# Cross-attention on one core: ten copies of the last batch's value tile move from VectorE to transfers of the sync engine

## The chip, the cores and the metric

One core of a Trainium2 chip runs the whole program in one launch. The metric is the time of an execution on the device in microseconds (us), lower is better. The engines are TensorE (PE in the profile; its weight loads are PEld), VectorE (DVE), ScalarE (ACT), GpSimd (POOL) and SyncE (SP, which only issues transfers). Each has its own instruction queue and works through it in order; semaphores tie them together.

## The reference

For each of 32 batches `x` and `y` (the context) are 256 x 1024, fp32, and all weights are 256 x 256:

```python
x_q = einsum('oc,bcn->bno', w_qk, y)
x_k = einsum('oc,bcn->bon', w_qk, x)
x_v = einsum('oc,bcn->bon', w_v, x) + b_v[None, :, None]
energy = einsum('bnc,bcm->bnm', x_q, x_k)
attention = softmax(energy, axis=-1)
attention = attention / (1e-07 + attention.sum(axis=1, keepdims=True))
x_r = einsum('bcn,bnm->bcm', x_v, attention)
x_r = relu(einsum('oc,bcn->bon', w_t, x - x_r) + b_t[None, :, None])
return x + x_r
```

## The kernel before

The weights are folded once at the start: `g` (w_qk transposed times w_qk) and `wvtT` (values and output projection in one). Every large product is a 2 x 2 block product of 128 x 512 blocks, done with seven block products in place of eight (class `Seven`: `p1` to `p7` are the products, `c11`, `c12`, `c21`, `c22` the combinations). The operands of the seven products are blocks of a tile and sums of blocks, and the sums are tiles of their own (`xs`, `ys`, `gt`, `us`, `et`).

One batch b has four stages:

- Keys (`Keys`, matmuls into `pg`): `gx` = g times x. GpSimd makes its block sums `gt`.
- Values (`Values`, matmuls into `pu`): `ut`, 128 x 2 x 2 x 512 fp32. The product that uses it needs it turned inside each 128 x 128 square. `turn` (line 366) transposes 32 x 32 squares with four VectorE instructions into `turned`; then each of the 16 pairs (partition group a, column group g) must be copied from one group of 32 partitions to another, back into `ut`. That copy is `move` (line 374): it takes the next `count` pairs off a list and issues one copy of 32 x 16 x 32 elements for each with whatever issuing function it is given. GpSimd then makes the block sums `us` in four instructions (`factors`, line 383), each 128 x 512.
- Energy (`Energy`, matmuls into `pe`), for t = 0 to 3: the energies of two row tiles go to `e` with their row minimum or maximum (custom VectorE instructions, `combine`, line 412), ScalarE takes the exponential (`exp`, line 436), and VectorE adds the rows, scaled, into `acc` (`share`, line 450). The 128 x 1024 `acc` instruction reads two tiles in SBUF. `columns` and `inverse` (lines 595 and 609) make the column factors `rc` of `acc`.
- Attention (`Attention`, matmuls into `po`): `e` times `rc` (`normal`), block sums `et` (`mix`), the products with `ut` and `us` (`epart`, line 489), and the output blocks `z`, stored by SP (`store`, line 505).

The stages of neighbouring batches overlap. The order of the instructions on PE, DVE, ACT and POOL is that of the program text (`InOrder`, lines 66 to 82, hangs each instruction behind the one before it on its engine); SP's transfers are put by the tile scheduler. The value tile of batch b+1 is made and turned at the end of batch b's attention (`now.run(un)`, line 783; its last call is `u.turn()`, line 571). The 16 copies are shared out in three ways:

- first batch: all 16 by SP transfers, line 680
- batches 1 to 30: eight by VectorE (line 790), eight by ScalarE (lines 670 and 684)
- batch 31, the last: twelve by VectorE (line 790, called at the end of batch 30's pass) and four by ScalarE (line 722, in t = 0 of batch 31's energies)

The matmuls of batch 31 that wait for these tiles are in `run` (line 533): `epart(self.one, 1)`, line 548, is the first to read the copied part of `ut_31`, and `epart(self.three, 2)`, line 550, comes after it; the sums `us_31` are first read by `epart(self.two, 5)`, line 551. In between lie all four steps of batch 31's energies, `columns` and `inverse`. In the last batch no loads are left.

The names used below: `pe` and `po` are PSUM banks of energies and attention; `ep1s`, `ep5s` and `ew` are ScalarE's copies of a bank that PE then adds onto; `nm` and `bias` are row extremes; `ri` is the reciprocal of a row sum. Almost every line of an engine with `InOrder` shows as L77, so instructions are told apart by their tiles.

Of the kernel before, what the change touches and what calls it, by code (L numbers as in the profile page):

```python
# [16 lines left out]
def kernel(  # L17
# [29 lines left out]
    nc = tc.nc  # L47
    B, C, N = x.shape
# [33 lines left out]
    pe, dve, act, pool = (InOrder(g) for g in (nc.tensor, nc.vector, nc.scalar, nc.gpsimd))  # L82
# [6 lines left out]
    def load(tag, b, pieces=1):  # L89
        from_, p = (x, xp) if tag == "x" else (y, yp)  # L90
        to = p.tile([P, KC, N], F32, tag=tag, name=f"{tag}_{b}")
        from_ = from_[b].rearrange("(k p) n -> p k n", p=P)
        W = KC // pieces
        for j in range(pieces):
            nc.sync.dma_start(to[:, ts(j, W)], from_[:, ts(j, W)])
        loaded[tag, b] = to
# [127 lines left out]
    def summed(tag, b):  # L224


        p = up if tag == "x" else one
        s = p.tile([P, 4, MB], F32, tag=f"{tag}s", name=f"{tag}s_{b}")
        t1, t3, t4, t2 = (s[:, j] for j in range(4))
        to = loaded[tag, b]  # L230
        b11, b12 = to[:, 0, ts(0, MB)], to[:, 0, ts(1, MB)]
        b21, b22 = to[:, 1, ts(0, MB)], to[:, 1, ts(1, MB)]
        if b == 0:
            pool.tensor_tensor(t1, b11, b12, ALU.add)
            pool.tensor_tensor(t2, b22, t1, ALU.add)
            pool.tensor_tensor(t3, b12, b22, ALU.add)
            pool.tensor_tensor(t4, b21, t2, ALU.add)
            steps = []
        else:
            from_ = (x if tag == "x" else y)[b]  # L240
            q = quarters(from_)
            nc.sync.dma_start(s[:, :2], q[:, 0, 1:2, :].to_broadcast([P, 2, MB]))
            nc.sync.dma_start(s[:, 2:], q[:, 1])
            steps = [
                lambda: accumulate(s[:, :2], corners(from_)),
                lambda: accumulate(s[:, 2:], s[:, 0:1].to_broadcast([P, 2, MB])),
                lambda: accumulate(t4, q[:, 1, 1]),
            ]
        return (b11, b21, b22, t4, t1, t2, t3), steps
# [345 lines left out]
    def columns(b):  # L595

        dve.tensor_reduce(
            parts[:, :, 0],
            acc.rearrange("p (j r) -> p j r", r=G32),
            AX.X,  # L600
            ALU.add,
            apply_transpose=True,
        )
# [5 lines left out]
    def inverse(b):  # L609


        sc = one.tile([P, NB, 1], F32, tag="sc", name=f"sc_{b}")
        s = sc[:, :, 0]
        for a in range(1, NG):
            moved(parts[:G32, :, a], parts[ts(a, G32), :, 0])
        dve.tensor_reduce(s[:G32], parts[:G32], AX.X, ALU.add)
        dve.reciprocal(s[:G32], s[:G32])
        moved(s[G32 : 2 * G32], s[:G32])
        moved(s[2 * G32 :], s[: 2 * G32])
        rc = one.tile([P, NB, G32], F32, tag="rc", name=f"rc_{b}")  # L620
        dve.transpose(rc.rearrange("p j r -> p (j r)"), sc.to_broadcast([P, NB, G32]))
        return rc.rearrange("p j r -> p (j r)")
# [27 lines left out]
    u = Values(0, xr)  # L650
# [11 lines left out]
    for b in range(B):  # L662
        more = b + 1 < B
        pair = []

        for t in range(HT):
            now = Energy(b, t, lhs, rhs)
            pair.append(now)
            if t == 0 and b > 0 and more:
                u.move(5, act.copy)  # L670
            now.p1()
            if t > 0:
                pair[t - 1].exp(1)
            now.p5()
            if t == 0:
                if b == 0:
                    u.p4()
                    u.c21()
                    u.turn()
                    u.move(16, nc.sync.dma_start)  # L680
                    xsteps[1]()
                    xsteps[2]()
                elif more:
                    u.move(3, act.copy)
                    before.end()
                    before.c21()
                    load("x", b + 1)
                e = ep.tile([P, NT, N], F32, tag="e", name=f"e_{b}")
                acc = one.tile([P, N], F32, tag="acc", name=f"acc_{b}")
                if before is not None:  # L690

                    pool.tensor_copy(behind, before.t4[:, HT - 1, :1])
                for step in gsteps:
                    step()
                if more:
                    ur, usteps = u.factors()
                    for step in usteps:
                        step()
            if t > 1:
                pair[t - 2].share(0)  # L700
            if t == 0:
                now.p6()
            now.p2()
            now.c11()
            if t == 1:
                pair[0].scale(1)
            if t > 1:
                pair[t - 1].share(1)
            if t > 0:
                now.p6()  # L710
            if t == 1:
                act.activation(acc, e[:, HT, :], AF.Copy, scale=scales[HT])
            if t > 0:
                pair[t - 1].p4()
                pair[t - 1].c21()
                pair[t - 1].exp(0)
            now.p3()
            now.c12()
            now.p7()
            now.c22()  # L720
            if t == 0 and not more:
                u.move(4, act.copy)
                ur, usteps = u.factors()
                for step in usteps:
                    step()
            elif t == 0 and b > 0:
                xn, xsteps = summed("x", b + 1)
            elif more and b > 0:
                xsteps[t - 1]()
        last = pair[-1]  # L730

        if more:
            g = Keys(b + 1, xn)
            g.p1()
        last.exp(1)
        if more:
            g.p5()
        else:
            before.xpart(before.one, 7, True)
        pair[2].share(0)  # L740
        last.p4()
        last.c21()
        last.share(1)
        if more:
            load("y", b + 1)
            rhs, ysteps = summed("y", b + 1)
            g.p6()
        else:
            before.epart(before.one, 7)
        last.exp(0)  # L750
        if more:
            g.p2()
            g.c11()
            g.p3()
        else:
            now = Attention(b, xr, ur)
            now.begin()
        last.share(0)
        columns(b)
        if more:  # L760
            g.p7()
            g.c12()
            g.c22()
            un = Values(b + 1, xn)
            un.p1()
            un.p5()
            un.p2()
            un.p6()
        else:
            before.c22()  # L770
        rc = inverse(b)
        if more:
            un.p3()
            g.p4()
            g.c21()
            un.p7()
            lhs, gsteps = g.factors()

        if more:
            now = Attention(b, xr, ur)  # L780
            now.begin()
            ysteps[0]()
            now.run(un)
            if b + 2 < B:
                now.xpart(now.one, 7, True)
                now.epart(now.one, 7)
                now.c22()
                now.put()
            now.put()
            un.move(8 if b + 2 < B else 12, dve.tensor_copy)  # L790
            ysteps[1]()
            ysteps[2]()
            before = now
            xr, u = xn, un
        else:
            before.end()
            now.run(None, before)
            now.finish()
# [30 lines left out]
```

## Time and profile before

| | |
|---|---|
| time, median of 3 runs | 2143.03 us (2142.68 to 2144.03) |
| the profiled execution's own time | 2142.41 us |
| its span (first to last instruction) | 2140.6 us, so 1.8 us lie around it |
| mean granted TensorE clock | 0.999 |
| ScalarE copies of `ut` | 244, median 615 ns |
| VectorE copies of `ut` | 252, median 417 ns |
| SP transfers of `ut` (first batch) | 16, issue 619 to 1668 ns, landing 2.7 to 5.4 us after issue |
| GpSimd instructions for `us` | 128, four to a batch |

A busy share is an average over the whole span. A single stage is read from the timeline: each line gives the start, the length, the engine, the line, the operation with its output and inputs, and how often it comes in a row; in square brackets stands the idle time of the engine before it and what ended it. One fp32 matmul of 128 x 128 by 128 x 512 is two MATMUL records, and at full clock one such pair starts 0.86 us after the last. `SPq` is SP's queue of transfers; a length there is the time to issue, not to move.

### The profile page before, as it was taken

Reading aid. Unit: us, or ns where it says so; the run is one execution under the profiler, and the core shown is the slowest. Engines: PE = TensorE matmul, PEld = TensorE weight load, DVE = VectorE, ACT = ScalarE, POOL = GpSimd, SP = SyncE. Lnnn points to the kernel's source line nnn. Section 1 sums busy time; section 2 is a strip of 40 time slices with the busy share of each in tenths; the row PEclk is TensorE's granted clock in tenths of the full one; section 3 lists DMA queues with packets and bytes.
Section 4 is the critical chain, followed back from the end, with each engine's and each line's share of the span. In section 5 each row is a group of like instructions: output and inputs, shape, how many; then the busy total and the mean of one; then the engine's idle time right before and its main releaser. Section 6 shows DMA issues by size and latency. Waiting matters only on the chain.

```text
span 2140.6 us, 17690 instructions
## 1 busy us (share of the span) xinstructions
PE 2130.6 (100%) x4972; PEld 941.3 (44%) x4972; DVE 1907.8 (89%) x3499; ACT 944.2 (44%) x1566; POOL 549.8 (26%) x487
## 2 busy tenths in 40 slices
PE   9999999999999999999999999999999999999999
PEld 5444444444444444444444444444444444444433
DVE  6899888998888988889888899888998888988898
ACT  5344554335543355433455344553345543355432
POOL 4322323222222122221222322323222222122220
PEclk9999999999999999999999999999999999999999
DMA  6445544445444454444554445554445444454420
GB/s 177 99 107 118 135 131 103 117 104 138 128 108 125 92 143 125 117 122 97 129 133 125 108 111 118 132 134 103 114 108 138 128 108 124 93 143 123 116 66 30
DMA packets 114210, 249.94 MB, mean 117 GB/s; under 512 B 17088, under 2 KB 17856, under 8 KB 114112
## 3 DMA queue, kind: packets, MB, share of 16 engines
q1 hardware_dynamic: 71456, 167.53, 23.6%
q0 software_dynamic: 42656, 81.28, 23.4%
q8 instruction: 40, 0.66, 0.1%
q14 instruction: 58, 0.48, 0.1%
HBM read 181.67 MB, written 33.55 MB: 101 GB/s over the span
## 4 chain that ended last, share of the span: by engine, by line
PE 97%; DVE 3%; issue 0%; ACT 0%; DVEq 0%
PE po L77 43%; PE pe L77 35%; PE pg L77 9%; PE pu L77 9%; DVE e L77 1%; DVE acc L77 0%; DVE et L77 0%; DVE ut L77 0%; PE idle L77 0%; DVE z L77 0%; DVE rc L77 0%; DVE parts L77 0%; DVE turned L77 0%; DVE sc L77 0%; DVE gx L77 0%
## 5 line engine op out<-in xcount | busy, mean ns | idle before, releaser
L77 PE MATMUL pe<-gt,ys 128*128 128x512 f32 x768 | 392.1, 592 | 0.0
L77 PE MATMUL po<-et,us 128*128 128x512 f32 x768 | 347.5, 594 | 1.1 <-DVE et L77 1.1
L77 DVE SCALAR_TENSOR_TENSOR e<-e,ri,rc 128x512 f32<-128x512 f32 x512 | 347.4, 747 | 1.1
L77 DVE SCALAR_TENSOR_TENSOR acc<-e,ri,acc 128x1024 f32<-128x1024 f32 x224 | 289.0, 1290 | 8.0
L77 PE MATMUL pe<-gx,y 128*128 128x512 f32 x512 | 261.4, 592 | 0.0
L77 PEld LDWEIGHTS pe<-gt,ys 128*128 128x128 f32 x768 | 146.0, 190 | 184.4 <-issue 182.6
L77 PEld LDWEIGHTS po<-et,us 128*128 128x128 f32 x768 | 143.1, 190 | 189.8 <-issue 145.9
L77 PE MATMUL po<-e,ut 128*128 128x512 f32 x512 | 224.9, 592 | 0.0
L77 ACT COPY ut<-turned 32x512 f32<-32x512 f32 x244 | 150.0, 615 | 157.4 <-DVE turned L77 154.6
L77 ACT ACTIVATE e<-e,nm 128x1024 f32<-128x1024 f32 x128 | 147.1, 1149 | 98.1 <-DVE nm L77 96.2
L77 POOL TENSOR_TENSOR gt<-gx 128x512 f32<-128x512 f32 x64 | 80.9, 1264 | 383.1 <-DVE gx L77 383.1
L77 DVE TENSOR_TENSOR et<-e 128x1024 f32<-128x1024 f32 x128 | 153.7, 1222 | 2.3
L77 PEld LDWEIGHTS po<-e,ut 128*128 128x128 f32 x512 | 97.3, 190 | 122.5 <-issue 99.0
L77 PEld LDWEIGHTS pe<-gx,y 128*128 128x128 f32 x512 | 97.3, 190 | 122.5 <-issue 122.2
L77 ACT ACTIVATE e<-e,bias 128x1024 f32<-128x1024 f32 x128 | 147.4, 1152 | 5.6 <-DVE bias L77 5.4
L77 DVE CUSTOM_DVE_ANT_0 e<-pe,ep1s 128x512 f32<-128x512 f32 x128 | 88.5, 691 | 64.1 <-ACT e L77 63.1
L77 PE MATMUL pe<-gx,ys 128*128 128x512 f32 x256 | 131.6, 596 | 3.5 <-DVE nm L77 3.5
L77 POOL TENSOR_TENSOR us<-ut 128x512 f32<-128x512 f32 x64 | 82.0, 1282 | 206.2 <-ACT ut L77 192.4
L77 PE MATMUL pe<-gt,y 128*128 128x512 f32 x256 | 131.7, 596 | 0.1
L77 ACT COPY ep1s<-pe 128x512 f32<-128x512 f32 x128 | 74.5, 582 | 114.5 <-PE pe L77 107.2
L77 PE MATMUL po<-e,us 128*128 128x512 f32 x256 | 120.5, 592 | 0.0
L77 DVE CUSTOM_DVE_ANT_0 e<-pe,zeros,nm 128x512 f32<-128x512 f32 x128 | 95.7, 748 | 27.3 <-PE pe L77 26.1
(118 smaller groups left out, 3200.4 us busy)
## 6 DMA issues: line engine op xcount, KB each, us to landing
y<-in_ctx_dram SPq DMA_DIRECT2D x32, 1024.0 KB, 4.9
out_dram<-z SPq DMA_DIRECT2D x128, 256.0 KB, 2.1
x<-in_x_dram SPq DMA_DIRECT2D x31, 1024.0 KB, 5.8
xs<-in_x_dram SPq DMA_DIRECT2D x62, 512.0 KB, 4.6
ys<-in_ctx_dram SPq DMA_DIRECT2D x62, 512.0 KB, 4.7
xs<-in_x_dram POOLq DMA_DIRECT2D x31, 512.0 KB, 6.3
xs<-xs POOLq DMA_DIRECT2D x31, 512.0 KB, 5.0
ys<-in_ctx_dram POOLq DMA_DIRECT2D x31, 512.0 KB, 6.2
```

The source lines that it names most:

```text
L77: self.last = getattr(self.engine, name)(*args, **kwargs)
```

## The change

In the last batch ten of the sixteen copies go from VectorE to SP. VectorE keeps two, ScalarE keeps its four. The other 31 batches are as before. In the compiled program PE, DVE, ACT and POOL keep their order, apart from the ten copies that are gone from DVE. SP gets ten transfers: one ahead of the store of output block z_0_1 of batch 30, nine behind it. The first `us` instruction of batch 31 on POOL, and the first matmul on PE that reads the moved part of `ut_31`, now wait for semaphores of transfers too.

```diff
@@ -720,6 +720,7 @@
             now.c22()
             if t == 0 and not more:
                 u.move(4, act.copy)
+                u.move(10, nc.sync.dma_start)
                 ur, usteps = u.factors()
                 for step in usteps:
                     step()
@@ -787,7 +788,7 @@
                 now.c22()
                 now.put()
             now.put()
-            un.move(8 if b + 2 < B else 12, dve.tensor_copy)
+            un.move(8 if b + 2 < B else 2, dve.tensor_copy)
             ysteps[1]()
             ysteps[2]()
             before = now
```

## The prediction

> **What bounds the kernel now.** The summary first: busy times of PE and DVE, and the engines of the chain of waits.
>
> ```profile
> PE 2130.6 (100%) x4972; PEld 941.3 (44%) x4972; DVE 1907.8 (89%) x3499; ACT 944.2 (44%) x1566; POOL 549.8 (26%) x487
> PE 97%; DVE 3%; issue 0%; ACT 0%; DVEq 0%
> ```
>
> TensorE bounds nearly everything, but 31 batches stay as they are, so only the 70 us after batch 31's value tile is turned count. Their timeline, without weight loads:
>
> ```profile
> 2070.24 2.50 ACT L77 COPY ut<-turned 32x512 f32<-32x512 f32 x4 [0.85 <-DVE turned L77]
> 2070.64 5.15 DVE L77 COPY ut<-turned 32x512 f32<-32x512 f32 x12
> 2073.75 1.02 PE L77 MATMUL pe<-gt,ys 128*128 128x512 f32 x2
> 2075.82 0.69 DVE L77 CUSTOM_DVE_ANT_0 e<-pe,ep1s 128x512 f32<-128x512 f32 x1
> 2078.08 1.82 PE L77 MATMUL pe<-gx,ys 128*128 128x512 f32 x2 [3.31 <-DVE nm L77]
> 2079.40 0.56 ACT L77 COPY ep5s<-pe 128x512 f32<-128x512 f32 x1
> 2080.01 1.99 PE L77 MATMUL pe<-gt,y 128*128 128x512 f32 x2
> 2081.84 1.02 PE L77 MATMUL pe<-gt,ys 128*128 128x512 f32 x2
> ```
>
> The reader is to see one stall. DVE copies for 5.15 us before it touches batch 31's energies; PE cannot overwrite a bank that DVE has not read, stands idle for 3.31 us, and then runs its next two products at half speed (1.82 and 1.99 in place of 1.02). The windows give the clock (length, busy times of PE, PEld, DVE, ACT and POOL, clock, transfers):
>
> ```profile
> 2074.00:2078.00 4.00, 0.78 (x2) 0.00 (x0) 3.77 (x11) 0.00 (x0) 1.99 (x2) 1.00 0.00 0
> 2078.40:2081.70 3.30, 3.19 (x4) 0.84 (x3) 1.41 (x5) 3.30 (x6) 2.61 (x3) 0.50 0.00 0
> ```
>
> From there the chain of waits, in order of time, goes PE, DVE, PE without slack:
>
> ```profile
> 2080.01 11.45 PE pe L77 x24
> ...
> 2105.94 6.72 DVE e L77 x10
> ...
> 2116.65 19.84 PE po L77 x44
> ```
>
> So what PE gains at 2081.84 reaches the end, unless DVE, saturated from 2091.59 on, is made later.
>
> **The ten copies that go.** Twelve start 2070.64 and the next instruction 2075.82: 5.18 / 12 = 0.432 each; ten are 4.32. The custom instruction moves from 2075.82 to 2071.50. Its inputs allow that: its matmul began at 2068.60, and ScalarE's last copy for t = 0 began at 2068.80 and took 0.59. The `nm` that frees PE moves from about 2078.0 to 2073.7.
>
> PE then has no such wait: the product of 2073.75 ends its slot at 2074.61, and the next follows at once. The one after, now at 2080.01, waits for `ep5s`, which stands on ACT behind the exponential, which waits for DVE's `bias`: the whole chain moves by 4.32, so this product starts at 2080.01 - 4.32 = 2075.69, against 2075.47 if PE were free to go. PE idles 0.22 us, not 3.31, so I take full clock: the slot after it is 0.86, not 1.83. The product at 2081.84 thus starts at 2075.69 + 0.86 = 2076.55, **5.29 us earlier**: 4.32 of copies and 0.97 of clock.
>
> **The ten transfers that come.** The first batch moves all sixteen so; these are SP's issues there and the time to land:
>
> ```profile
> 26.84 14.64 SPq L380 DMA_DIRECT2D ut<-turned  x16
> 40.85 0.63 SPq L380 DMA_DIRECT2D ut<-turned  x1
> DMA to landing us min/median/max: 2.7/3.8/5.4
> ```
>
> Where no other transfer runs they start 0.68 apart (39.49, 40.17, 40.85); beside GpSimd's accumulating loads it is 0.93 on average (14.0 / 15). In the last batch nothing else runs, so I take 0.68. First issue 0.09 after the last transpose ends (as in batch 0: 26.75 to 26.84), at 2070.24, for 0.75; then the store, 0.37, issued at 2071.04 instead of 2070.75; then nine, the last at 2071.43 + 8 x 0.68 = 2076.87. SP has nothing else until the next store at 2117.23, and the delayed store's buffer is next written at 2107.48, so 0.3 there costs nothing. With the landing times above the tile is whole by 2079.6 to 2082.3; its first matmul stands at 2107.28 - 5.29 = 2102.0. That is 20 us of cover at the worst landing, and PE's new wait is free.
>
> **POOL's four instructions, moved later, are the price.** They waited for DVE's copies (2075.93) and now wait for the landing. In batch 0 POOL began 3.20 us after the last issue (44.05 - 40.85), so 2076.87 + 3.20 = 2080.07. They end near 2086 and are needed at 2114.16 - 5.29 = 2108.9: no matter. What they run beside does matter. Batch 0 again:
>
> ```profile
> 44.05 2.13 POOL L77 TENSOR_TENSOR us<-ut 128x512 f32<-128x512 f32 x1 [7.72 <-DVE ri L77]
> 47.49 1.28 POOL L77 TENSOR_TENSOR us<-ut 128x512 f32<-128x512 f32 x1
> 47.52 2.33 DVE L77 SCALAR_TENSOR_TENSOR acc<-e,ri,acc 128x1024 f32<-128x1024 f32 x1
> 48.72 2.26 POOL L77 TENSOR_TENSOR us<-ut,us 128x512 f32<-128x512 f32 x1
> ```
>
> `acc` takes 1.28 alone and 2.33 here: begun just after a POOL instruction, it ended 1.08 after that one's end (48.77 to 49.85). POOL in turn waited for `acc` and ended about 1.13 after it. DVE's PSUM instructions beside POOL at 2075.93 to 2081.0 kept their 0.69 to 0.75, so in the kernel before these four cost nothing: that cover goes.
>
> Shift the `acc` instructions by 5.29: 2078.76, 2081.11, 2084.87, 2087.12. POOL's first, at 2080.07, ends by 2081.34 and delays the second `acc` by nothing to 0.03. POOL's second waits for that `acc` (2082.39) and ends at 2083.52; the third runs 2083.48 to 2084.75; the fourth starts at 2084.71, 0.16 ahead of the third `acc`, and ends at 2085.98. That `acc` ends 1.08 later, at 2087.06, not 2086.15: **0.91 lost**, of which 0.15 is covered by DVE's idle time before 2091.59. Net 0.76. The bounds over starts from 2079 to 2083.5, worked through the same way: 0 (POOL falls between `acc` instructions, as for 2082.4) and 1.76 (two `acc` caught early, as for 2081.05).
>
> The Trainium skill, "SBUF — State Buffer", section "Who interferes with whom", says that a VectorE instruction with two SBUF inputs and a GpSimd instruction that reads SBUF exclude each other for the whole instruction, whichever issues first. Whole instructions would make the loss 2085.98 - 2084.87 = 1.11 rather than 0.91, and the time 2138.7; the row of batch 0 shows 0.2 of overlap, and I go by the row. It speaks against the change: the copies that leave DVE come back as a lock. The skill's "DMA: Bandwidth & Descriptors", section "Specifications", asks for 512 B at least in a run, and these have 32 x 4 = 128 B; a slow transfer would only push POOL along the bounds above.
>
> **Sum.** 5.29 - 0.76 = 4.53. The profiled execution's 2142.41 (span 2140.6 and 1.8 around it) becomes 2137.88; it lies 0.62 under the median, so the median 2143.03 becomes **2138.5**. What a measurement of this kernel can tell from no change is about 0.2%, 4.29 us, so the line is 2138.74: the forecast sits just on the faster side.
>
> **Rivals.**
>
> *No collision.* POOL's fourth and the third `acc` are 0.16 apart; if DVE gets there first, nothing is lost: 2143.03 - 5.29 = 2137.7. For it: the small margin. Against: batch 0 has the same succession with a margin of 0.03 (47.49 against 47.52), and POOL won.
>
> *Two collisions.* The transfers land 0.5 to 1 us later than in my estimate. Two `acc` are caught: up to 1.76 lost, 2143.03 - 5.29 + 1.76 = 2139.5, within 0.2%. For it: batch 0's issues of up to 1.67 and landings of up to 5.4. Against: those met other transfers.
>
> *The clock stays low.* If 0.22 us of idle time still costs PE its clock, the 0.97 is not won: 2138.5 + 0.97 = 2139.5. Against: the 0.54 idle at 2116.1 is followed by pairs at no such length (in these windows 0.50 is seen only after 3.31).
>
> *The transfers are late: slower.* Were each to wait for the one before, at batch 0's longest landing of 5.4, the tile would be whole at 2070.24 + 54 = 2124.2; POOL and PE start 0.4 later, 17.3 after the present 2107.28: 2160.3. It decides from 3.7 us a transfer on. Against: batch 0's sixteen were through in 17.2 us (26.84 to 44.05).
>
> *The change does not do what it says*: the compiled order has ten transfers on SP and two copies on DVE, so no.
>
> **How the numbers follow.** Forecast 0.44, no collision 0.18, two collisions 0.22, low clock 0.09, late transfers or another loss 0.07. Of the forecast four fifths fall beyond 0.2%: faster 0.35 + 0.18 = 0.53; same 0.09 + 0.22 + 0.09 = 0.40; slower 0.07. The range runs from no collision less 0.4 (runs of before lie 0.35 under their median), 2137.3, to two collisions plus 0.8, 2140.3; most of the 0.07 is left out.
>
> **What would show it.** Two copies on DVE after 2070.64; no PE idle over 0.5 before 2100 and no clock of 0.50 there; the last transfer issued near 2076.9 and POOL's first `us` near 2080.1; one or two `acc` longer than 1.28. A PE wait on a transfer near 2102 would prove the forecast wrong, as would `po` still starting at 2107.28.

## The result and the profile after

| | before | changed |
|---|---|---|
| median, 11 runs each | 2142.81 us (2141.7 to 2145.11) | 2137.98 us (2136.71 to 2138.78) |
| ratio, 95% interval | | 0.9976 (0.9968 to 0.9984) |
| profiled execution, span | 2140.6 | 2136.2 |
| stage: first transpose of the last value tile to the end of the span | 72.93 | 68.41 |
| of it, up to the start of the last 44 `po` matmuls | 48.98 | 44.49 |

The change makes the kernel 4.83 us faster in the medians, 0.23%; the interval reaches from 0.16% to 0.32%, so the times alone do not put it beyond 0.2%. The last two rows are cleaner. Two profiled executions that run the same instructions up to batch 31 reach it up to 2.2 us apart (its first transpose starts at 2065.82 in one run below and 2068.04 in another), so from here on each stage is measured from its own first transpose: 2140.6 - 2067.67 before, 2136.2 - 2067.79 after. The difference is 4.52.

The end of the span varies too. From the start of the last 44 `po` matmuls, the last link of the chain of waits, VectorE's last instruction starts 19.93 or 19.94 later in every run below, but the end of the span, with the last stores, comes 23.7 to 24.0 later. So small differences are read up to the start of these matmuls: 2116.65 - 2067.67 = 48.98 before, 2112.28 - 2067.79 = 44.49 after. That difference is 4.49.

The timeline of the changed kernel where the stall was, PE and one copy of ACT (start, length, engine, operation):

```profile
2073.88 1.02 PE L77 MATMUL pe<-gt,ys 128*128 128x512 f32 x2
...
2074.74 1.02 PE L77 MATMUL pe<-gx,ys 128*128 128x512 f32 x2
...
2075.21 0.56 ACT L77 COPY ep5s<-pe 128x512 f32<-128x512 f32 x1
...
2075.83 1.12 PE L77 MATMUL pe<-gt,y 128*128 128x512 f32 x2
...
2076.79 1.02 PE L77 MATMUL pe<-gt,ys 128*128 128x512 f32 x2
```

The product that stood idle for 3.31 us follows its predecessor at once (2073.88, 2074.74). The next waits for `ep5s`, as worked out, and none takes twice its time. The window of the old stall has the clock at 1.00 and the transfers at 97 GB/s:

```profile
2074.00:2078.00 4.00, 3.93 (x10) 1.51 (x9) 2.40 (x9) 3.94 (x6) 0.00 (x0) 1.00 0.62 97
```

What is given back stands in the timelines of three engines of the changed kernel. First SP's queue, with the ten transfers and the store between them:

```profile
2070.42 0.60 SPq L380 DMA_DIRECT2D ut<-turned  x1
2071.11 0.57 SPq L506 DMA_DIRECT2D out_dram<-z  x1
2071.73 6.03 SPq L380 DMA_DIRECT2D ut<-turned  x9
```

GpSimd's sums, which waited for them:

```profile
2079.53 1.88 POOL L77 TENSOR_TENSOR us<-ut 128x512 f32<-128x512 f32 x1 [9.54 <-ACT ep1s L77]
2081.49 2.27 POOL L77 TENSOR_TENSOR us<-us,ut 128x512 f32<-128x512 f32 x1
2083.72 1.27 POOL L77 TENSOR_TENSOR us<-ut 128x512 f32<-128x512 f32 x1
2084.95 1.28 POOL L77 TENSOR_TENSOR us<-ut,us 128x512 f32<-128x512 f32 x1
```

And `acc` on VectorE. The third one of the kernel before:

```profile
2090.16 1.28 DVE L77 SCALAR_TENSOR_TENSOR acc<-e,ri,acc 128x1024 f32<-128x1024 f32 x1
```

And the second to fourth of the changed kernel:

```profile
2081.34 1.28 DVE L77 SCALAR_TENSOR_TENSOR acc<-e,ri,acc 128x1024 f32<-128x1024 f32 x1
...
2085.11 2.20 DVE L77 SCALAR_TENSOR_TENSOR acc<-e,ri,acc 128x1024 f32<-128x1024 f32 x1
...
2088.03 1.28 DVE L77 SCALAR_TENSOR_TENSOR acc<-e,ri,acc 128x1024 f32<-128x1024 f32 x1
```

The third `acc` starts 0.16 after GpSimd's fourth sum and takes 2.20 in place of 1.28. (GpSimd's first sum is put down to ScalarE's `ep1s`, which ended just before it, at 2079.30, but which the sums do not read. The last transfer was issued at 2077.1 and is due at about 2079.4 by the median landing of 2.3; in e1 below, without the transfers, the first sum starts at 2070.96, right behind ScalarE's copies of `ut`.) The end of the chain of waits, after: `2112.28 19.85 PE po L77 x44`, where it was 2116.65.

### The profile page after: what moved, and what is told of

It is laid out like the page before. It is cut to its first block, busy times and chain, and to the rows that moved or that the text cites. A ratio compares the mean times of both kernels' runs of the same rounds, so it can differ in the third digit from the quotient of the medians.

```text
span 2136.2 us, 17699 instructions
## 1 busy us (share of the span) xinstructions
PE 2128.9 (100%) x4972; PEld 941.1 (44%) x4972; DVE 1904.5 (89%) x3489; ACT 944.8 (44%) x1566; POOL 551.4 (26%) x487
## 4 chain that ended last, share of the span: by engine, by line
PE 97%; DVE 2%; issue 0%; ACT 0%; DVEq 0%
PE po L77 44%; PE pe L77 36%; PE pg L77 9%; PE pu L77 9%; DVE e L77 1%; DVE acc L77 0%; DVE et L77 0%; PE idle L77 0%; DVE parts L77 0%; DVE rc L77 0%; DVE sc L77 0%; DVE gx L77 0%; PE pw L77 0%; DVE z L77 0%; DVE ut L77 0%
## 5 line engine op out<-in xcount | busy, mean ns | idle before, releaser
L77 PE MATMUL pe<-gt,ys 128*128 128x512 f32 x768 | 392.2, 592 | 0.0
L77 PE MATMUL po<-et,us 128*128 128x512 f32 x768 | 347.5, 594 | 1.1 <-DVE et L77 1.1
L77 DVE SCALAR_TENSOR_TENSOR e<-e,ri,rc 128x512 f32<-128x512 f32 x512 | 347.4, 746 | 1.1
L77 DVE SCALAR_TENSOR_TENSOR acc<-e,ri,acc 128x1024 f32<-128x1024 f32 x224 | 289.9, 1294 | 8.0
L77 PE MATMUL pe<-gx,y 128*128 128x512 f32 x512 | 261.5, 592 | 0.0
L77 PEld LDWEIGHTS pe<-gt,ys 128*128 128x128 f32 x768 | 145.8, 190 | 183.9 <-issue 182.2
L77 PEld LDWEIGHTS po<-et,us 128*128 128x128 f32 x768 | 143.1, 190 | 189.9 <-issue 145.9
L77 PE MATMUL po<-e,ut 128*128 128x512 f32 x512 | 224.9, 592 | 0.0
L77 ACT COPY ut<-turned 32x512 f32<-32x512 f32 x244 | 150.0, 615 | 157.4 <-DVE turned L77 154.5
L77 ACT ACTIVATE e<-e,nm 128x1024 f32<-128x1024 f32 x128 | 147.1, 1149 | 98.7 <-DVE nm L77 96.8
L77 POOL TENSOR_TENSOR gt<-gx 128x512 f32<-128x512 f32 x64 | 80.8, 1262 | 384.4 <-DVE gx L77 384.4
L77 DVE TENSOR_TENSOR et<-e 128x1024 f32<-128x1024 f32 x128 | 153.7, 1222 | 2.3
L77 PEld LDWEIGHTS po<-e,ut 128*128 128x128 f32 x512 | 97.3, 190 | 122.5 <-issue 99.0
L77 PEld LDWEIGHTS pe<-gx,y 128*128 128x128 f32 x512 | 97.3, 190 | 122.5 <-issue 122.0
L77 ACT ACTIVATE e<-e,bias 128x1024 f32<-128x1024 f32 x128 | 147.4, 1152 | 1.3 <-DVE bias L77 1.1
L77 DVE CUSTOM_DVE_ANT_0 e<-pe,ep1s 128x512 f32<-128x512 f32 x128 | 88.5, 691 | 64.1 <-ACT e L77 62.9
L77 POOL TENSOR_TENSOR us<-ut 128x512 f32<-128x512 f32 x64 | 82.8, 1293 | 208.4 <-ACT ut L77 192.5
L77 PE MATMUL pe<-gx,ys 128*128 128x512 f32 x256 | 130.8, 593 | 0.9 <-DVE nm L77 0.9
L77 PE MATMUL pe<-gt,y 128*128 128x512 f32 x256 | 130.8, 593 | 0.1
L77 ACT COPY ep1s<-pe 128x512 f32<-128x512 f32 x128 | 74.6, 582 | 113.7 <-PE pe L77 106.3
L77 PE MATMUL po<-e,us 128*128 128x512 f32 x256 | 120.5, 592 | 0.0
L77 DVE CUSTOM_DVE_ANT_0 e<-pe,zeros,nm 128x512 f32<-128x512 f32 x128 | 95.7, 747 | 27.3 <-PE pe L77 26.1
```

What stands on the lines that cost most here:

```text
L77: self.last = getattr(self.engine, name)(*args, **kwargs)
```

## The experiments

All stages below run from the first transpose of the last value tile to the end of the span, of one profiled execution each; "to `po`" is the part up to the start of the last 44 `po` matmuls, and the differences are taken there. The clock is that up to the last matmul.

| run | stage | to `po` | against changed | clock in the stage | longest acc |
|---|---|---|---|---|---|
| before | 72.93 | 48.98 | +4.49 | 0.50 for 3.4 us | 1.28 |
| changed | 68.41 | 44.49 | 0 | 1.00 | 2.20 |
| e1_left_out | 67.78 | 43.82 | -0.67 | 1.00 | 1.29 |
| e2_pool_late | 68.16 | 44.23 | -0.26 | 1.00 | 1.29 |
| e3_sums_moved | 74.95 | 50.94 | +6.45 | 0.50 for 6.8 us | 2.19 |
| e4_kept_busy | 72.12 | 48.13 | +3.64 | 1.00 | 1.29 |
| e5_five | 71.40 | 47.67 | +3.18 | 0.50 for 3.4 us | 1.29 |
| e6_pool_last_acc | 67.72 | 43.81 | -0.68 | 1.00 | 1.29 |
| e7_twelve | 67.18 | 43.48 | -1.01 | 1.00 | 1.29 |
| e8_sums_busy | 72.83 | 48.80 | +4.31 | 1.00 | 2.20 |
| e9_five_busy | 69.65 | 45.97 | +1.48 | 1.00 | 1.28 |

### What the sums on GpSimd cost: e1, e2, e6

e1_left_out, against the changed kernel:

```diff
-                u.move(10, nc.sync.dma_start)
+                u.moves = u.moves[10:]
```

> The changed kernel with its ten moved copies left out altogether: no transfers for them and no copies, so part of the last batch's value tile stays unturned. Theory (the gain is 5.2 us of stall taken off TensorE, less 0.7 that the block sums on GpSimd cost where they run beside acc): GpSimd's sums start near 2073 instead of 2079.5, end before the first acc, every acc of the last batch takes 1.28, and the span is 0.7 below the changed kernel's 2136.2, at 2135.4 to 2135.6. Rival (the lock costs nothing at the end, because the 0.9 of the long acc is covered): span 2136.1 to 2136.3.

No `acc` is long, and the way to `po` is 0.67 shorter. The expected span, 2135.4 to 2135.6, was missed at 2133.6, because that execution reached batch 31 some 2 us earlier; measured from the stage's own start, the 0.7 that was expected is there. So the transfers and what follows from them cost 0.67 in all. e2 keeps the transfers and takes the collision away:

```diff
                 ur, usteps = u.factors()
-                for step in usteps:
-                    step()
...
         last.share(0)
+        if not more:
+            pool.tensor_copy(behind, acc[:, :1])
+            for step in usteps:
+                step()
         columns(b)
```

> The changed kernel with its ten transfers, and GpSimd's four block sums of the last batch held back until the last acc is done. Theory: no acc is over 1.30, the sums run in 2096 to 2101.5 beside instructions that read one tile in SBUF, and the span falls by 0.7 to 2135.4 to 2135.6 (median near 2137.3). Rival (transfers, not the sums, hold DVE up or the long acc is covered): 2136.1 to 2136.3. A second rival: the sums end too late and push the first e<-e,ri,rc instruction, span 2136 to 2137.

Every `acc` is short, but only 0.26 is won: the second rival of the expectation was right. The sums end at 2101.77, beside the first `e<-e,ri,rc` instructions, which read two tiles in SBUF as well. In e2's timeline, GpSimd's last sum:

```profile
2100.50 1.27 POOL L77 TENSOR_TENSOR us<-ut,us 128x512 f32<-128x512 f32 x1
```

and VectorE's first ten instructions of that kind:

```profile
2101.14 7.14 DVE L77 SCALAR_TENSOR_TENSOR e<-e,ri,rc 128x512 f32<-128x512 f32 x10
```

The ten take 7.14 in place of 6.71: the collision has moved, and 0.43 of it is back on the path (0.26 + 0.43 = 0.69). e6 starts the sums one `acc` earlier, so that they end as the ten begin:

```diff
-            pool.tensor_copy(behind, acc[:, :1])
+            pool.tensor_copy(behind, scales[HT - 1])
```

> The changed kernel with GpSimd's four sums of the last batch held until the reciprocal ahead of the last acc, about 1.2 earlier than in e2_pool_late, whose sums met the first e<-e,ri,rc instructions and lengthened ten of them from 6.71 to 7.14. Theory: every acc takes 1.28 to 1.30, the ten take 6.7 to 6.75, and the stage from the first transpose of the last value tile to the end is 67.7 to 67.9, like e1_left_out's 67.8 and 0.6 under the changed kernel's 68.4. Rival (0.25 is all there is, as e2_pool_late's 68.16 has it): 68.1 to 68.2.

67.72, as expected: with all ten transfers in place the way to `po` is as short as without any (43.81 and 43.82). VectorE's ten instructions take 6.71 again. The transfers are free; what they cost the changed kernel is when GpSimd runs.

### The same sums in the kernel before: e3 and e8

e3 is the kernel before with its sums started where the changed kernel has them:

```diff
             if t > 1:
                 pair[t - 2].share(0)
+            if t == 2 and not more:
+                pool.tensor_copy(behind, scales[0])
+                for step in usteps:
+                    step()
```

> The kernel before, all twelve copies on VectorE and no transfers, with GpSimd's four block sums started just after the reciprocal ahead of the first acc, as they start in the changed kernel. Theory: the third acc (or the second and third) takes about 2.2, and the span rises by about 0.7 from 2140.6 to 2141.2 to 2141.6. Rival: the sums cost nothing there, 2140.5 to 2140.7.

One `acc` takes 2.19, the second and not the third. But the way to `po` grew by 1.96, not by 0.7, and both accounts of the experiment are too small. PE's timeline shows the rest:

```profile
2077.37 2.07 PE L77 MATMUL pe<-gx,ys 128*128 128x512 f32 x2 [3.31 <-DVE nm L77]
2079.30 2.08 PE L77 MATMUL pe<-gt,y 128*128 128x512 f32 x2
2081.16 1.92 PE L77 MATMUL pe<-gt,ys 128*128 128x512 f32 x2
2082.87 1.42 PE L77 MATMUL pe<-gx,y 128*128 128x512 f32 x2
```

The idle time is the old 3.31, but four products run slow where there were two. The windows have the clock at 0.50 in both halves:

```profile
2077.00:2080.20 3.20, 2.83 (x3) 1.00 (x4) 2.01 (x8) 2.67 (x5) 0.00 (x0) 0.50 0.00 0
2080.30:2083.60 3.30, 3.30 (x5) 1.35 (x4) 1.18 (x3) 1.61 (x3) 0.00 (x0) 0.50 0.00 0
```

From the first slow product to the second product of t = 2 the kernel before needs 5.48 (2078.08 to 2083.56), e3 6.76 (2077.37 to 2084.13): 1.28 more, and 1.96 - 1.28 = 0.68 is left for the long `acc`. e8 tests that by keeping PE busy in the same kernel, with the edit of e4 below:

> e3_sums_moved with the four repeated products of e4_kept_busy, so that TensorE keeps its clock. Stages as before, from the first transpose of the last value tile to the end: e4_kept_busy has 72.1, e3_sums_moved 74.9. Theory (of e3_sums_moved's 2.0 over the kernel before 1.3 is a half clock that held two periods of 3.41 instead of one, and 0.7 is the long acc): one acc near 2.2, clock 1.00 throughout, stage 72.7 to 72.9. Rival (the moved sums cost the whole 2.0): 74.0 or more.

72.83, as expected, with the clock at 1.00 and one long `acc` on VectorE, the third:

```profile
2088.50 2.20 DVE L77 SCALAR_TENSOR_TENSOR acc<-e,ri,acc 128x1024 f32<-128x1024 f32 x1
```

Up to `po`, e8 has 48.80 against e4's 48.13: the moved sums cost 0.67. Measured four ways (e1 0.67, e6 0.68, e3 0.68, e8 0.67) the collision costs 0.67 to 0.68.

### What the clock is worth: e4, e5, e9

e4 is the kernel before with PE kept at work through the stall, by computing one product again into the same bank:

```diff
             now.p2()
+            if t == 1 and not more:
+                for _ in range(4):
+                    now.product(now.three, 2)
             now.c11()
```

> The kernel before, with one product of the last batch's second step computed four times more into the same bank, in the place where TensorE stands idle for 3.3 us; the copies and the wait stay. Theory (0.97 of the gain is the clock): the granted clock stays at 1.00, the product beside p3 takes 0.86 instead of 1.83, and the span falls by 0.9 to 1.0, to 2139.6 to 2139.8. Rival (the half clock is hidden behind ScalarE's copy and DVE): 2140.5 to 2140.7.

```profile
2077.39 1.13 PE L77 MATMUL pe<-gx,ys 128*128 128x512 f32 x2
2079.32 1.12 PE L77 MATMUL pe<-gt,y 128*128 128x512 f32 x2 [0.81 <-ACT ep5s L77]
2080.28 1.02 PE L77 MATMUL pe<-gt,ys 128*128 128x512 f32 x2
```

That is PE's timeline of e4. All copies and the wait on VectorE are still there; the slot after the `ep5s` wait is 0.96, not 1.83, and the way to `po` is 0.85 shorter (expected were 0.9 to 1.0). The clock's share is real and separate from the copies. e5 moves half of the ten:

```diff
-                u.move(10, nc.sync.dma_start)
+                u.move(5, nc.sync.dma_start)
...
-            un.move(8 if b + 2 < B else 2, dve.tensor_copy)
+            un.move(8 if b + 2 < B else 7, dve.tensor_copy)
```

> The changed kernel with five transfers and seven VectorE copies in the last batch in place of ten and two. All numbers are for the stage from the first transpose of the last batch's value tile to the end of the span, which is 72.9 in the profile of the kernel before and 68.4 in the changed one. Theory (the clock falls only after an idle stretch of the old length, and copies count 0.43 each): five copies are 2.16; TensorE idles some 1.3, keeps a clock of 1.00, and wins the 0.9 of the half-speed products as well; GpSimd's sums start near 2076.5, end near 2081.5 and meet at most the first acc, which has slack behind it. Stage 69.8 to 70.0. Rival (the gain is spread evenly over the copies): half of 4.5, stage 70.7. Rival (the clock still falls): 70.8 or more.

The expectation failed: 71.40, not 69.9. Two idle stretches of 1.15 and 0.81 were enough for the half clock, as PE's timeline of e5 has it:

```profile
2075.96 1.12 PE L77 MATMUL pe<-gx,ys 128*128 128x512 f32 x2 [1.15 <-DVE nm L77]
2077.90 1.66 PE L77 MATMUL pe<-gt,y 128*128 128x512 f32 x2 [0.81 <-ACT ep5s L77]
2079.35 1.92 PE L77 MATMUL pe<-gt,ys 128*128 128x512 f32 x2
2081.06 1.38 PE L77 MATMUL pe<-gx,y 128*128 128x512 f32 x2
```

Its windows before and after the clock falls (columns as in the windows of before):

```profile
2075.00:2078.30 3.30, 1.53 (x3) 0.59 (x4) 2.40 (x9) 2.17 (x5) 2.29 (x2) 1.00 0.11 18
2078.40:2081.70 3.30, 3.30 (x5) 1.35 (x4) 1.09 (x3) 2.11 (x3) 2.62 (x3) 0.50 0.00 0
```

In 2075.0 to 2078.3 PE worked for 1.53 of 3.30, and then got half its clock for the next 3.4. e9 is e5 with the product repeated twice, which leaves 0.51 of idle time before the `ep5s` product:

> e5_five with one product repeated twice, which leaves TensorE some 0.7 of idle time in place of 2.0; the copies stay five and seven. Theory (e5_five's 71.4 missed 69.9 by the half clock alone): the clock stays 1.00 and the stage falls to 69.6 to 69.8. Rival (five copies are worth 1.6 whatever the clock does): 71.2 to 71.4.

69.65, clock 1.00, with the slot after the `ep5s` wait at 0.97 (2077.24 to 2078.21). So e5 missed by the clock alone, which cost it 1.70 (47.67 against 45.97), and the copies count 0.43 each, as in the sum: e9 lies 2.16 under e4, with five copies fewer and the clock at 1.00 in both. The profiled execution of e5 was one of its two longest (2140.82; the ten runs have 2138.1 to 2139.4 and then 2140.82 and 2141.17), and its median, 2138.97, is no worse than e9's 2139.19. The mean granted clock recorded for each of its runs says what the others did: 0.999 in these two and 1.0 in the other eight. 3.4 us at half clock lower the mean by 0.0008. So eight of the ten kept their clock, as the expectation had it, and the trace is of one of the two that lost it.

### A better version: e7

e6 with the last two VectorE copies given to SP as well:

```diff
-                u.move(10, nc.sync.dma_start)
+                u.move(12, nc.sync.dma_start)
...
-            un.move(8 if b + 2 < B else 2, dve.tensor_copy)
+            un.move(8 if b + 2 < B else 0, dve.tensor_copy)
```

> As e6_pool_last_acc, and the last two VectorE copies go to SP as well: twelve transfers. Theory: VectorE's first energy instruction starts 0.85 earlier, TensorE no longer idles before the product that waits for ep5s, and 0.3 more is won: stage 67.4 to 67.5, median near 2137.0. Rival (two transfers more delay something, or TensorE is bound by ScalarE there): 67.8.

In PE's timeline of e7 no wait is left at these products:

```profile
2073.76 1.02 PE L77 MATMUL pe<-gx,ys 128*128 128x512 f32 x2
2074.62 1.02 PE L77 MATMUL pe<-gt,y 128*128 128x512 f32 x2
2075.48 1.02 PE L77 MATMUL pe<-gt,ys 128*128 128x512 f32 x2
```

The way to `po` is 1.01 shorter than in the changed kernel: 0.68 for the sums, as in e6, and 0.33 for the two copies and the wait on `ep5s`, where 0.3 was expected. (The stage of 67.18 is 1.23 shorter; the other 0.2 lies behind the matmuls, where executions differ by as much.) The median is 2136.52 against 2142.79, ratio 0.9971 (0.9959 to 0.9982). It is the shortest of all, though by its times it cannot be told from the changed kernel (0.9976, 0.9968 to 0.9984): the way to `po` says it is faster.

## Why the prediction was right

It forecast 2138.5 against 2143.03, that is 4.53 faster; measured were 4.83 in the medians, 4.52 in the stage and 4.49 up to `po`. Term by term, with after's times set back by the 0.12 that its stage starts later:

| term | predicted | measured |
|---|---|---|
| ten copies, at the `ep5s` product | 4.32 | 4.30 (2080.01 to 2075.83 - 0.12) |
| full clock, slot after it | 0.97 | 0.87 (1.83 to 0.96) |
| together, at the product of 2081.84 | 5.29 | 5.17 (to 2076.79 - 0.12) |
| last transfer issued | 2076.87 | 2077.1 - 0.12 |
| GpSimd's first sum | 2080.07 | 2079.53 - 0.12 |
| length of the third acc | 2.19 (1.28 + 0.91) | 2.20 |
| net price of the sums | 0.76 | 0.68 (5.17 - 4.49); 0.67 and 0.68 by e1 and e6 |

**The copies.** Counting 0.43 for each, with the wait handed on through `nm`, `bias`, the exponential and `ep5s`, was right to 0.02; e9 has it again with five copies (2.15 at the `ep5s` product, 5 x 0.43).

**The clock.** Its size was right for this pair of profiles, 0.87 for 0.97 (the first pass after the short wait for `ep5s` still takes 0.10 more), and e4 has it by itself as 0.85. The reason given, a short idle time instead of a long one, was too simple: e5 lost the clock after two idle times of 1.15 and 0.81, and in e3 the half clock lasted twice as long after the same stall of 3.31. So 0.97 was the price in the profiled execution, not a fixed one, and that this execution was a cheap one is luck. Of 68 further runs of the kernel before, recorded beside the experiments, 42 have a mean granted clock of 0.999 and 26 of 0.998; e3's profile, with 6.8 us at half clock, has 0.998. The medians of the two groups are 2142.60 and 2143.41. So more than a third of the runs probably lose the clock for 6.8 us, and this may be why the medians differ by 4.83 and the stages by 4.49; no trace of such a run of the kernel before was taken.

**The transfers.** The spacing of 0.67 (6.03 / 9) was taken right, and nothing waits for them on PE. They landed sooner than batch 0's rows suggested: the median is 2.3 from issue to landing, against 3.8 there. It did not matter, because the first sum then met the first `acc` and waited for it, which brought the succession back to the worked one: fourth sum 0.16 ahead of the third `acc`, as forecast. That the waits restored it is luck: the prediction had worked out no meeting with the first `acc`, and its bounds for other starts ran from 0 to 1.76. The net price is 0.08 under the forecast mainly because VectorE's next instruction started at 2087.24, 0.07 ahead of the recorded end of the long `acc` (2085.11 + 2.20), where the prediction let it wait for that end.

**The rivals.** No collision (2137.7) is excluded by the 2.20. Two collisions are excluded: one `acc` is long. The low clock did not come, though e5 shows how near it is. The late transfers fell: the last sum ended at 2086.23, over 20 us before its use.

## What to carry to other kernels

When an engine is relieved, ask which other engine's work is moved by it, and beside what it will then run: here the transfers were free, and the only price was that GpSimd's four sums met an instruction of VectorE that reads two tiles in SBUF. Delaying the sums without looking moved the same collision to the next such instruction (e2); putting them into the gap won 0.68 (e6). And compare short stages from their own start, and up to their last wait: here executions differ by up to 2.2 us before the stage and by up to 0.3 behind its last wait, and the effects in it are of that size.

## What the runs showed of the hardware

**The clock of TensorE goes by periods of 3.41 us.** In the traces' records of the granted clock the time from its first rise to its first fall is 2071.89 in before, e3 and e5 alike (6.49 to 2078.38 in before, 6.46 to 2078.35 in e5). The clock stays down for 3.413 in before and e5 and for 6.827, twice that, in e3, and falls again 58.03 after it rose, behind the last matmul. 58.03 is 17 times 3.4133, and 2071.89 is 607 times that. In the other eight kernels the first fall comes 2129.92 or 2133.33 after the rise, 624 or 625 times that.

Counted by these periods, PE was busy for 0.30 of 3.41 ahead of the fall in before, for 0.63 in e3, and for 1.58 in e5; with 2.61 (e4) and 3.16 (e9) the clock stayed. The sum of the busy time alone does not decide: in the periods in which the last matmuls end, 1.25 (e9) and 1.35 (e8) were followed by a fall and 1.43 (e6) was not, though it is less than e5's 1.58. What decides in between stays open. The way up goes by the same periods: half clock ended after a period with 3.30 (before) or 3.41 busy (e5), and went on after one with 2.88 (e3, where PE began its work 0.53 after the fall).

This agrees with the Trainium skill, "TensorE: Matmul & The Clock Gate", section "What's actually happening", which tells of a window of 3.41 us that runs freely; it gives a whole idle window as the cause, and there e5 differs: PE was busy for 1.58 us of the period before the fall, and neither of its idle times, 1.15 and 0.81, fills a window.

**An `acc` and a sum on GpSimd exclude each other, but by these records not for the whole instruction.** An `acc` begun 0.16 after a sum of 1.28 took 2.20; a wait for the whole sum would have made it 2.40. The row of batch 0 had shown the same 0.2 of overlap. The profile's times on GpSimd are rough, so the 0.2 may lie in the record of the sum's end.

**Transfers of 128 B runs cost about 0.67 us of SP each and land in 2.3** where only one store moves beside them, and in 3.8 in the first batch beside other transfers.
